# Layer 0: four of the six block sums of a group made by GpSimd from blocks on chip, in place of adding DMAs

## The chip, the cores and the metric

The kernel runs on one core of a Trainium2 chip. The core has a matrix engine (TensorE, PE in the profile), three engines that work on data in the on-chip memory SBUF (VectorE is DVE, ScalarE is ACT, GpSimd is POOL), a queue engine that issues DMAs (SyncE, SP), and 16 DMA engines. Matmuls write into a second memory, PSUM. The engines run side by side, each through its own list of instructions in order, and wait for each other by semaphores. The metric is the device time of one execution in microseconds. The kernel before takes 595.17 us, the median of three runs (594.85 to 595.21).

## The reference, cut to what matters

Four layers are applied to x of 8 batches, 256 tokens and 1024 features, each added to its input.

```python
x = x + L0(x)   # x @ W^T, plus 2 * gated low-rank experts (router, top 2 of 8)
x = x + L1(x)   # x @ W1^T + b + coeff[b] * (x @ (2*mask[b] - 1))
x = x + L2(x)   # x @ weight[id[b]]^T
x = x + L3(x)   # low rank, A[id[b]] and B[id[b]]
```

The change concerns layer 0 alone. Its main part is

```python
base = jnp.einsum('btd,od->bto', x, W)
h = jnp.einsum('btd,erd->bter', x, A)
lora_out = jnp.einsum('bter,bte,eor->bto', h, gates, B)
return base + SCALING * lora_out
```

## The kernel before, in words

**Precision.** All operands are float32. Each is split into a high part, rounded to the type that the matrix engine takes (fp32r), and a low part, the rest. A product is made as high by high, high by low and low by high. ScalarE makes the high part (the tile whi, line 304) and VectorE subtracts it from the source to make the low part (wlo, by the helper at line 69, called from `lows`, line 307). Line 69 is VectorE's two-operand helper, so nearly all of VectorE's work shows under it.

**Groups and Strassen's scheme.** The 8 batches are 4 pairs of 512 tokens. Layer 0 takes two pairs at a time, so there are two groups (g = 0 and 1). In a group the product W by x is a 2 by 2 block product with seven block multiplications in place of eight (Winograd's form of Strassen's method). A11 to A22 are the quadrants of W, with the identity added where a block lies on the diagonal (that adds x itself), and B11 to B22 those of x: the first index halves the features, the second is the pair. Eight sums are needed for the multiplications:

- S1 = A21 + A22, S2 = A11 - S1 (the opposite sign of the usual form, and T2 likewise), S3 = S2 + A22, S4 = A12 + S2,
- T1 = B12 - B11, T2 = T1 - B22 (made by VectorE, like S2), T3 = B22 - B12, T4 = T2 + B21.

S2 and T2 are VectorE subtractions. The six that the title counts are the others, S1, S3, S4, T1, T3 and T4. Every sum takes the memory of a block that is no longer needed (the dictionary in `quad`, line 197): S1 and S3 lie in A21, S2 in A11, S4 in A12, T1 in B11, T3 in B12, T2 and T4 in B21.

**How a sum is made before.** A DMA issued by GpSimd adds an array of HBM to a tile in SBUF (`add`, line 748, the accumulating form). For S3 and S4 ScalarE first copies S2 to the place (lines 757 and 762), for T1 and T3 it negates the block there (line 768). Then the DMA adds the other operand, read from HBM once more. For S1 and S3 GpSimd adds the identity to diagonal 128x128 blocks (`fold_quad`, `fold_block`, line 251). Each sum has two halves (h = 0, 1) of 128x1024 elements, and each half is one DMA of 512 KB. The adding DMAs are the queue q0 of the page.

**Slots.** The order of the work is written out by hand; the framework adds the waits. Group g has 16 slots in layer 0, two per entry of a list of products, the h of each being the half of the inner dimension:

```python
L0_PRODUCTS = [("A11", "B11"), ("A12", "B21"), None, ("S1", "T1"), ("S4", "B22"),
               ("S2", "T2"), ("S3", "T3"), ("A22", "T4")]
```

The third entry has no product: its slots (4 and 5) take B12 and B22 through the experts alone. A slot consists of `l0_slot`, which issues the evacuations of PSUM (`l0_evacuate`), then the high parts of blocks two slots ahead (HI_AHEAD = 4 items), the folds, the low parts of blocks about one and a half slots ahead (LO_AHEAD = 3), the extra work listed for the slot, and then the matmuls (`l0_main`). A block of weights and one of x are the two items of a slot. There are 5 buffers for high parts and 4 for low parts, so a part can't be made before the slot that frees its buffer is over. Seven evacuations bring the results from PSUM; some of them (VectorE additions of PSUM tiles to SBUF tiles, c in the profile) have to be done before the next slot may write the same tile.

The extra work is listed by `l0_works` with `at(s, ...)`: the sums; the router of a pair (13 small VectorE instructions, `router`, line 331); the weighing of the experts (`weigh`); gates brought to the layout of the matmuls by the TensorE (for p0 of group 0) or through HBM (`expand`, `gates_by_rank`); their high and low parts (ghi, glo, `split_gates`, line 420). p0 and p1 are the two pairs of a group. T1 is listed in slot 2 of group 0 and slot 1 of group 1, S4 in slot 4, T3 in slots 6 and 4, S3 in slot 7, T4 in slots 9 and 10. Entries with a negative number come either ahead of the slot's other work or, in `l0_mids`, behind its matmuls: in slot 3 of group 0 the router of p1 and the second half of S2.

**Queues.** SyncE issues the loads in the order in which they are written. GpSimd's queue holds the folds, the adding DMAs of layer 0 and some adding DMAs of layer 1 (line 281). In one queue an instruction that waits holds up all behind it.

After layer 0 of a group come layers 1, 2 and 3 of its two pairs (`unit_slot`), about 180 us of matmuls for group 0 before layer 0 of group 1.

Of the kernel before, what the change touches and what calls it, by code (L numbers as in the profile page):

```python
# [12 lines left out]
ALU = mybir.AluOpType  # L13
# [21 lines left out]
def kernel(ctx: ExitStack, tc: tile.TileContext, x, lang, coeff, ids,  # L35
# [14 lines left out]
    nc = tc.nc  # L50
# [15 lines left out]
    copy = nc.scalar.copy  # L66

    def tt(o, a, b, op):
        nc.vector.tensor_tensor(o, a, b, op)  # L69
# [99 lines left out]
    for g in range(2):  # L169
        s = 0  # L170
        for pr in L0_PRODUCTS:
            for h in range(2):
                if pr is None:
                    quad = ("B12", "B22")[h]
# [16 lines left out]
    def pair_of(g, j):  # L191
        return 2 * g + 1 - j
# [4 lines left out]
    def quad(g, name):  # L197

        where = {"S1": "A21", "S2": "A11", "S3": "A21", "S4": "A12",
                 "T1": "B11", "T2": "B21", "T3": "B12", "T4": "B21"}.get(name, name)  # L200
        if where[0] == "A":
            return [W0[g, where, h] for h in range(2)]
        i, j = int(where[1]) - 1, int(where[2]) - 1
        return [X[g][:, j, 4 * i + 2 * h:4 * i + 2 * h + 2, :] for h in range(2)]
# [48 lines left out]
    def fold_quad(t, h, eng=None):  # L253
        for k in range(2):
            c = (2 * h + k) * P
            fold_block(t[:, k, c:c + P], eng)
# [30 lines left out]
    flat = lambda ap: ap.rearrange("p a b -> p (a b)")  # L287
# [43 lines left out]
    def router(pairs):  # L331
        n4 = 4 * len(pairs)
        t = lambda nm, w: gp.tile([P, n4, w], F32, tag=nm, name=nm)
        lt = t("lt", 32)
        for i, p in enumerate(pairs):
            nc.vector.transpose(flat(lt[:, 4 * i:4 * i + 4]), pls.pop(p)[:, :P])
        lv = t("lv", E)
        np = len(pairs)
        tt(lv.rearrange("p (q n) e -> p q n e", q=np),
           lt.rearrange("p (q n) e -> p q n e", q=np)[:, :, :, :E],  # L340
           bias[:, pairs[0]:pairs[0] + np].rearrange("p q (o e) -> p q o e", o=1)
           .to_broadcast([P, np, 4, E]), ALU.add)
        revb = rev.to_broadcast([P, n4, E])

        def top(v, nm):
            mx = t(f"mx{nm}", 1)
            nc.vector.tensor_reduce(mx, v, AX.X, ALU.max)
            eq = t(f"eq{nm}", E)
            tt(eq, v, mx.to_broadcast([P, n4, E]), ALU.is_equal)
            tt(eq, eq, revb, ALU.mult)  # L350
            fi = t(f"fi{nm}", 1)
            nc.vector.tensor_reduce(fi, eq, AX.X, ALU.max)
            oh = t(f"oh{nm}", E)
            tt(oh, revb, fi.to_broadcast([P, n4, E]), ALU.is_equal)
            return mx, oh

        m1, oh1 = top(lv, "1")
        rest = t("rest", E)
        nc.vector.scalar_tensor_tensor(rest, oh1, -3.0e38, lv, ALU.mult, ALU.add)
        m2, oh2 = top(rest, "2")  # L360
        d = t("d", 1)
        tt(d, m2, m1, ALU.subtract)
        routed[tuple(pairs)] = lt, d, oh1, oh2

    def weigh(pairs):

        n4 = 4 * len(pairs)
        t = lambda nm, w: gp.tile([P, n4, w], F32, tag=nm, name=nm)
        lt, d, oh1, oh2 = routed.pop(tuple(pairs))
        ex = t("ex", 1)  # L370
        nc.scalar.activation(ex, d, AF.Exp)

        den = t("den", 1)
        nc.vector.tensor_scalar(den, ex, 1.0, 0.5, ALU.add, ALU.mult)
        wt1 = t("wt1", 1)
        nc.vector.reciprocal(wt1, den)
        wt2 = t("wt2", 1)
        tt(wt2, wt1, ex, ALU.mult)
        tt(oh1, oh1, wt1.to_broadcast([P, n4, E]), ALU.mult)
        tt(oh2, oh2, wt2.to_broadcast([P, n4, E]), ALU.mult)  # L380
        tt(lt[:, :, :E], oh1, oh2, ALU.add)
        for i, p in enumerate(pairs):
            gate4 = lt[:, 4 * i:4 * i + 4]
            if p == pair_of(0, 0):
                gxs[p] = gp.tile([P, 4 * E, R], F32, tag="lg", name=f"gx{p}", bufs=3)
                nc.vector.tensor_copy(gxs[p].rearrange("p (n e) r -> p n e r", n=4),
                                      gate4[:, :, :E].rearrange("p n (e o) -> p n e o", o=1)
                                      .to_broadcast([P, 4, E, R]))
                continue
            gxs[p] = gp.tile([P, P], F32, tag=f"gx{i}", name=f"gx{p}")  # L390
            nc.vector.transpose(gxs[p], flat(gate4))
# [3 lines left out]
    def expand(p):  # L395

        by_expert[p] = dram.tile([E, N], F32, tag=f"gates{p}", name=f"gates{p}")
        gx = gxs.pop(p)
        for g in range(4):
            nc.sync.dma_start(by_expert[p][:, g * P:(g + 1) * P], gx[32 * g:32 * g + E])  # L400
# [13 lines left out]
    def gates_by_rank(p):  # L414

        gts[p] = gp.tile([P, N], F32, tag="lg", name=f"gt{p}", bufs=3)
        src = by_expert.pop(p).rearrange("e (o t) -> e o t", o=1).to_broadcast([E, R, N])
        nc.sync.dma_start(gts[p], src)

    def split_gates(key, gt):  # L420
        hi = gp.tile([P, N], FR, tag="ghi", name="ghi", bufs=2)
        lo = gp.tile([P, N], FR, tag="glo", name="glo", bufs=2)
        copy(hi, gt)
        tt(lo, gt, f32(hi), ALU.subtract)
        gates[key] = hi, lo

    def gate(p):
        tt(gts[p], phs.pop(p), gts[p], ALU.mult)

    def gate_difference(g):  # L430

        a, b = (gts.pop(pair_of(g, j)) for j in range(2))
        tt(a, a, b, ALU.subtract)
        split_gates(("diff", g), a)
# [289 lines left out]
    def sub(g, o, a, b, h):  # L724
        q = [flat(quad(g, n)[h]) for n in (o, a, b)]
        tt(q[0], q[1], q[2], ALU.subtract)
# [12 lines left out]
    def l0_works(g):  # L739


        p0, p1 = pair_of(g, 0), pair_of(g, 1)
        w = {}

        def at(s, *fs):
            w.setdefault(s, []).extend(fs)

        def add(name, h, src):
            nc.gpsimd.dma_start(quad(g, name)[h], src, accum_op=ALU.add)

        def s1_add(h):
            fold_quad(quad(g, "S1")[h], h)
            add("S1", h, w0[1, 2 + h])

        def s3_add(h):
            t = quad(g, "S3")[h]
            copy(flat(t), flat(quad(g, "S2")[h]))
            fold_quad(t, h)
            add("S3", h, w0[1, 2 + h])

        def s4_add(h):
            copy(flat(quad(g, "S4")[h]), flat(quad(g, "S2")[h]))
            add("S4", h, w0[0, 2 + h])

        def less(h, name, j, i):

            t = flat(quad(g, name)[h])
            nc.scalar.mul(t, t, -1.0)
            add(name, h, x[pair_of(g, j)][:, 4 * i + 2 * h:4 * i + 2 * h + 2])

        def both(f, *args):
            return [lambda h=h: f(h, *args) for h in range(2)]

        def subs(o, a, b):
            return [lambda h=h: sub(g, o, a, b, h) for h in range(2)]

        def lb_parts():
            copy(lbs[0], lb_raw)
            tt(lbs[1], lb_raw, f32(lbs[0]), ALU.subtract)

        if g == 0:
            at(1, constants, *both(s1_add))
            at(2, *both(less, "T1", 1, 0), lambda: router([p0]))
            at(3, lambda: weigh([p0]), lb_parts, lambda: sub(0, "S2", "A11", "S1", 0))
            at(4, *both(s4_add), lambda: gate(p0))
        else:
            at(0, *both(s1_add))
            at(1, *both(less, "T1", 1, 0))
            at(3, *subs("S2", "A11", "S1"))
            at(4, *both(s4_add), lambda: gate(p0))  # L790
        at(-5 if g else 4, lambda: split_gates(p0, gts[p0]))
        if g == 0:
            at(5, lambda: weigh([p1]), lambda: expand(p1))
        else:
            at(1, lambda: router([p1, p0]))
            at(2, lambda: weigh([p1, p0]), lambda: expand(p0), lambda: expand(p1))
            at(3, lambda: gates_by_rank(p0))
        at(6, lambda: gates_by_rank(p1))
        at(4 if g else 6, *both(less, "T3", 1, 1))
        t2 = subs("T2", "T1", "B22")  # L800
        at(7, t2[0], *both(s3_add))
        at(-8, lambda: gate(p1))
        at(8, lambda: split_gates(p1, gts[p1]), t2[1])
        at(10, lambda: gate_difference(g))
        for h in range(2):
            at(9 + h, lambda h=h: add("T4", h, x[p0][:, 4 + 2 * h:6 + 2 * h]))
        for i in range(4):
            at(12 + i, lambda i=i: split_c(p1, i))
        return w
# [328 lines left out]
    b = NB - 1  # L1138
    at, xt = l3[b // 2], xts[b]
# [88 lines left out]
```

## Time and profile before

| what | value |
|---|---|
| median of three runs | 595.17 us |
| the profiled execution | 595.89 us |
| its span (first to last instruction) | 594.0 us |
| TensorE busy | 586.2 us, 3388 matmuls |
| VectorE busy | 468.5 us, 561 instructions |
| ScalarE busy | 379.0 us, 449 instructions |
| GpSimd busy | 127.2 us, 178 instructions |
| layer 0 of group 0, matmuls | about 5 to 110 us |
| layer 0 of group 1, matmuls | about 292 to 398 us |
| DMA, queue of SyncE (q1) | 112.14 MB |
| DMA, queue of GpSimd (q0) | 16.78 MB |
| granted TensorE clock | 0.999 |

A row of the list in order of time reads: start in us, busy us, engine, line, operation, output<-inputs, shape, count, and in brackets how long the engine was idle before it and what ended that. In the names, A is a quadrant of W or a sum in its place, x a block of x or a sum in its place, c the result area of layer 0 (at first it also holds raw low-rank weights), lb a part of the experts' second matrix, ph the PSUM tile of the experts' first product, mm and po the PSUM tiles of layer 0 and of layers 1 and 2.

### The profile page before, as it was taken

How to read it: one execution, taken by the hardware profiler on the slowest of the kernel's cores; microseconds unless marked ns; L12 is line 12 of the kernel's file. 1: busy time of each engine (PE TensorE's matmuls, PEld its weight loads, DVE VectorE, ACT ScalarE, POOL GpSimd, SP SyncE). 2: the span in 40 equal slices, each digit the busy share in tenths (PEclk: the TensorE clock that was granted, in tenths of full speed). 3: DMA queues.
4: the chain of work that ended last, by engine and by line, in shares of the span. 5: the costliest groups of instructions: out<-in, count | busy, mean ns of one | idle time of the engine just before them, and what ended most of it. 6: DMA issues, size and time to landing. Idle time of an engine off the chain costs nothing.

```text
span 594.0 us, 9230 instructions
## 1 busy us (share of the span) xinstructions
PE 586.2 (99%) x3388; PEld 501.3 (84%) x3388; DVE 468.5 (79%) x561; ACT 379.0 (64%) x449; POOL 127.2 (21%) x178
## 2 busy tenths in 40 slices
PE   9999999999999999999999999999999999999995
PEld 8878788888888888888888888888888888888884
DVE  7687788899689999586647786889977999976753
ACT  5658466687659887544544865668866789864331
POOL 2313170113121013112210234211422210511000
PEclk9999999999999999999999999999999999999999
DMA  8977994567685876499913799835858586845704
GB/s 292 345 169 156 222 273 146 199 242 261 199 287 178 302 265 244 167 352 346 276 26 98 165 271 237 236 108 212 311 176 271 198 292 223 317 144 184 224 1 141
DMA packets 39878, 130.02 MB, mean 219 GB/s; under 512 B 4922, under 2 KB 6682, under 8 KB 39066
## 3 DMA queue, kind: packets, MB, share of 16 engines
q1 hardware_dynamic: 34938, 112.14, 54.0%
q0 software_dynamic: 4608, 16.78, 15.1%
q8 instruction: 26, 0.43, 0.3%
q10 hardware_dynamic: 288, 0.52, 0.3%
q14 instruction: 18, 0.15, 0.1%
HBM read 120.99 MB, written 8.44 MB: 218 GB/s over the span
## 4 chain that ended last, share of the span: by engine, by line
PE 88%; DMA 7%; DVE 2%; issue 1%; SPq 1%; ACT 0%; DVEq 0%; ACTq 0%
PE po L663 60%; PE mm L663 22%; DMA c<-in_lb 2%; DMA gt<-gates 2%; DMA A<-in_w 1%; DVE wlo L69 1%; DMA c<-in_la 1%; PE pb L473 1%; PE pf L502 1%; PE ph L692 1%; PE ph L693 1%; PE pl L326 1%; PE ph L694 1%; DMA gates<-gx 0%; PE pb L540 0%
## 5 line engine op out<-in xcount | busy, mean ns | idle before, releaser
L663 PE MATMUL po<-hl,whi 128*128 128x512 f32 x1016 | 243.7, 391 | 0.0
L663 PEld LDWEIGHTS po<-hl,whi 128*128 128x128 f32 x1016 | 186.4, 188 | 35.8
L69 DVE TENSOR_TENSOR wlo<-raw,whi 128x1024 fp32r<-128x1024 f32 x128 | 159.1, 1250 | 8.0 <-issue 7.5
L304 ACT CAST whi<-raw 128x1024 fp32r<-128x1024 f32 x128 | 133.7, 1047 | 19.1 <-PE mm L663 8.0
L663 PEld LDWEIGHTS po<-hl,wlo 128*128 128x128 f32 x1016 | 130.7, 191 | 6.2 <-issue 1.2
L663 PE MATMUL po<-hl,wlo 128*128 128x256 f32 x1016 | 133.1, 283 | 0.0
L663 PE MATMUL mm<-whi,whi 128*128 128x512 f32 x224 | 87.8, 392 | 0.0
L663 PE MATMUL mm<-wlo,whi 128*128 128x512 f32 x224 | 87.2, 390 | 0.0
L273 ACT ACTIVATE raw<-raw,negc,c 128x1024 f32<-128x1024 int32 x64 | 79.5, 1243 | 10.5 <-DMA raw<-in_mask 10.3
L251 POOL TENSOR_TENSOR raw<-raw,ident 128x128 f32<-128x128 f32 x72 | 54.3, 756 | 125.7 <-DMA raw<-in_w 115.7
L69 DVE TENSOR_TENSOR raw<-raw,w 128x1024 f32<-128x1024 f32 x56 | 69.5, 1240 | 1.1 <-issue 1.1
L663 PE MATMUL mm<-whi,wlo 128*128 128x512 f32 x224 | 70.3, 389 | 0.0
L251 POOL TENSOR_TENSOR w<-w,ident 128x128 f32<-128x128 f32 x28 | 27.7, 990 | 165.1 <-DMA w<-in_w 126.9
L69 DVE TENSOR_TENSOR wlo<-x,whi 128x1024 fp32r<-128x1024 f32 (+1 forms) x38 | 44.1, 1170 | 13.4 <-PE mm L663 8.5
L636 ACT COPY c<-po 128x512 f32<-128x512 f32 (+1 forms) x34 | 18.8, 553 | 52.5 <-PE po L663 52.4
L663 PEld LDWEIGHTS mm<-whi,whi 128*128 128x128 f32 x224 | 42.2, 188 | 9.7 <-issue 0.8
L663 PEld LDWEIGHTS mm<-whi,wlo 128*128 128x128 f32 x224 | 42.0, 188 | 8.9
L663 PEld LDWEIGHTS mm<-wlo,whi 128*128 128x128 f32 x224 | 42.1, 188 | 8.5
L304 ACT CAST whi<-A 128x1024 fp32r<-128x1024 f32 x26 | 27.3, 1050 | 28.4 <-PE mm L663 18.5
L304 ACT CAST whi<-x 128x1024 fp32r<-128x1024 f32 x34 | 35.3, 1049 | 10.8 <-PE mm L663 9.1
L639 ACT ACTIVATE sum<-po,b_sb 128x512 f32<-128x512 f32 (+1 forms) x36 | 23.1, 642 | 29.6 <-PE po L663 29.6
L69 DVE TENSOR_TENSOR wlo<-A,whi 128x1024 fp32r<-128x1024 f32 (+3 forms) x37 | 37.5, 1028 | 4.5 <-ACT whi L304 4.4
(134 smaller groups left out, 492.5 us busy)
## 6 DMA issues: line engine op xcount, KB each, us to landing
raw<-in_mask SPq DMA_DIRECT2D x64, 512.0 KB
raw<-in_w SPq DMA_DIRECT2D x64, 512.0 KB
w<-in_w SPq DMA_DIRECT2D x28, 512.0 KB
out<-c SPq DMA_DIRECT2D x29, 256.0 KB
A<-in_w SPq DMA_DIRECT2D x14, 512.0 KB
x<-in_x SPq DMA_DIRECT2D x6, 1024.0 KB
A<-in_w POOLq DMA_DIRECT2D x12, 512.0 KB, 9.1
x<-in_x POOLq DMA_DIRECT2D x12, 512.0 KB, 9.2
```

The source lines that it names most:

```text
L69: nc.vector.tensor_tensor(o, a, b, op)
L251: (eng or nc.gpsimd).tensor_tensor(t, t, ident, ALU.add)
L273: nc.scalar.activation(f32(raws[n]), raws[n], AF.Identity, bias=negc[:, b:b + 1], scale=c2[:, b:b + 1])
L304: copy(prep_hi(i), flat(source(i)))
L326: mm(pls[p][32 * g:32 * g + 32, :P], wrs[:, k, :], X[a][:, j, k, g * P:(g + 1) * P], start=(k == 0), stop=(k == K - 1))
L473: mm(pb[c:c + 32, j * T:(j + 1) * T], l3b[b][:, k, :], xts[b][:, k, :], start=(k < 4), stop=(k >= 4))
L502: mm(po, l3[q][:, (m + i) * P:(m + i + 1) * P], rt, start=True, stop=True)
L636: copy(xs, po[:, :, T:])
L639: nc.scalar.activation(xs, po[:, :, T:], AF.Identity, bias=b1c)
L663: mm(*args, skip_group_check=True, **kw)
L692: mm(phs[p], hi, v[0][:, kk], start=(k == 0), stop=False)
L693: mm(phs[p], hi, v[1][:, kk], start=False, stop=False)
```

## The change

S3, S4, T1 and T3 are no longer made by a ScalarE pass and an adding DMA. One GpSimd tensor_tensor for each half makes the sum from two blocks that lie in SBUF: S3 = S2 + A22, S4 = A12 + S2 (in A12's own place), T1 = B12 - B11, T3 = B22 - B12. In both groups together that is 16 GpSimd instructions of 128x1024, in place of 16 ScalarE passes and 16 DMAs of 512 KB. S1 and T4 stay adding DMAs. S3's folds stay behind it, on GpSimd. The slots in which the sums are listed are unchanged.

```diff
+        def on_chip(o, a, op, b):
+            nc.gpsimd.tensor_tensor(*(flat(t) for t in (o, a, b)), op)
+
         def s3_add(h):
             t = quad(g, "S3")[h]
-            copy(flat(t), flat(quad(g, "S2")[h]))
+            on_chip(t, quad(g, "S2")[h], ALU.add, quad(g, "A22")[h])
             fold_quad(t, h)
-            add("S3", h, w0[1, 2 + h])
 
         def s4_add(h):
-            copy(flat(quad(g, "S4")[h]), flat(quad(g, "S2")[h]))
-            add("S4", h, w0[0, 2 + h])
-
-        def less(h, name, j, i):
-
-            t = flat(quad(g, name)[h])
-            nc.scalar.mul(t, t, -1.0)
-            add(name, h, x[pair_of(g, j)][:, 4 * i + 2 * h:4 * i + 2 * h + 2])
+            t = quad(g, "S4")[h]
+            on_chip(t, t, ALU.add, quad(g, "S2")[h])
+
+        def block_less(h, name, other):
+
+            t = quad(g, name)[h]
+            on_chip(t, quad(g, other)[h], ALU.subtract, t)
...
         if g == 0:
...
-            at(2, *both(less, "T1", 1, 0), lambda: router([p0]))
+            at(2, *both(block_less, "T1", "B12"), lambda: router([p0]))
...
         else:
...
-            at(1, *both(less, "T1", 1, 0))
+            at(1, *both(block_less, "T1", "B12"))
...
-        at(4 if g else 6, *both(less, "T3", 1, 1))
+        at(4 if g else 6, *both(block_less, "T3", "B22"))
```

## The prediction

> **What bounds the kernel.** I read the page's busy times first, then who waited for whom on TensorE, then the chain that ended last.
>
> ```profile
> PE 586.2 (99%) x3388; PEld 501.3 (84%) x3388; DVE 468.5 (79%) x561; ACT 379.0 (64%) x449; POOL 127.2 (21%) x178
> ```
>
> The waits of TensorE (us in total, times, longest):
>
> ```profile
> PE mm L663 <- ACT ghi L423: 0.3, 1, 0.3
> PE po L1155 <- DVE rt L451: 0.2, 1, 0.2
> ```
>
> The matmul stream has no hole: of 594.0 us TensorE is busy 586.2, and the rest is the first 1.1 us and the tail after 586. Inside, the waits view names one wait of 0.3 us in layer 0 and one of 0.2 us at the end. So work taken off ScalarE or the DMA queues can shorten the span by about 0.3 us plus hardly visible waits, some 0.5 us in all. It can lengthen it wherever something TensorE reads becomes late, and each such delay stays to the end, since a full stream never catches up. The question is how much spare time the feeding engines have at the places the change touches. The rows of group 0 in order of time, in the middle of layer 0, answer it (start, duration in us; wlo is the low half of a block made by VectorE, read by the matmuls as the third product):
>
> ```profile
> 31.76 1.05 ACT L778 CAST lb<-c 128x1024 fp32r<-128x1024 f32 x1 [1.78 <-DMA c<-in_lb]
> ...
> 38.11 1.22 DVE L69 TENSOR_TENSOR A<-A,A 128x1024 f32<-128x1024 f32 x1
> 39.24 2.35 DVE L69 TENSOR_TENSOR wlo<-x,whi 128x1024 fp32r<-128x1024 f32 x2
> ...
> 40.51 0.50 PE L693 MATMUL ph<-wlo,laghi 128*128 128x512 f32 x1
> ...
> 43.70 0.50 PE L663 MATMUL mm<-glo,lb 128*128 128x512 f32 x1
> ```
>
> The first wlo of 39.24 ends at about 40.4, and the matmul that reads it starts at 40.51 and shows 0.50 where its neighbours show 0.39 or 0.40. The low gates (glo, ended 43.65) are taken at 43.70, again with 0.50. VectorE is exactly on time here, with no reserve; in 24 to 48 us it is busy 20.2 of 24.
>
> **What goes.** Per group eight ScalarE passes (L757, L762, L768; median 1.04 to 1.05 us each, 8.4 us) and eight adding DMAs of 512 KB (POOL queue, 0.87 us to issue, 9.1 us median to landing). ScalarE was waiting in these stretches, and the summed blocks were ready before their casts. These removals are worth 0, and 0.3 us where the gates of p1 land at 61.6, with S3 and T3 adding beside them.
>
> **What comes.** Per group eight GpSimd tensor_tensor of 128x1024 f32. S3's folds and the S1 and T4 adds stay. The trace has no such instruction; its nearest row is the fold, 128x128, on the same engine:
>
> ```profile
> 19.88 0.89 POOL L251 TENSOR_TENSOR A<-A,ident 128x128 f32<-128x128 f32 x2 [8.08 <-DMA A<-in_w]
> ```
>
> 0.44 us for 128 elements; eight of these make at most 3.5 us. As GpSimd time this is harmless: that engine is busy 3.7 us of the 24 from 24 to 48, its other work there is one row of DMA issues after another, and an adding DMA took about 9 us. What matters is what it does to VectorE. Another stretch:
>
> ```profile
> 84.12 2.75 POOL L251 TENSOR_TENSOR A<-A,ident 128x128 f32<-128x128 f32 x2
> ...
> 85.08 1.48 DVE L69 TENSOR_TENSOR wlo<-A,whi 128x1024 fp32r<-128x1024 f32 x1
> 86.48 1.48 DVE L69 TENSOR_TENSOR hl<-c,hl 128x1024 fp32r<-128x1024 f32 x1
> 87.89 1.48 DVE L69 TENSOR_TENSOR wlo<-x,whi 128x1024 fp32r<-128x1024 f32 x1
> 89.29 1.21 DVE L69 TENSOR_TENSOR wlo<-A,whi 128x1024 fp32r<-128x1024 f32 x1
> ```
>
> Two folds that took 0.89 alone take 2.75, and each of three folds (the third starts at 86.84) lengthens one VectorE instruction by 0.26 us. They take turns. The instruction at 54.84, which reads PSUM and one SBUF operand, kept its 1.22 us under two folds. The Trainium skill ("SBUF — State Buffer", who interferes with whom) has the rule: a VectorE instruction with two SBUF inputs and a GpSimd one that reads SBUF exclude each other for the whole instruction. That speaks against the change: costed as hidden GpSimd time it is worth 0; by the rule each instruction also costs VectorE its hold. The hold: 0.26 us for 128 elements gives 2.1 us for 1024. The skill's "GPSIMD Engine Reference" (performance versus the Vector engine) has 4497 ns for 2048 elements, so an estimate of 2.25; the upper bound is the 3.5 above, the lower 0 (VectorE always first). I take 2.1, which both support.
>
> **Where it falls, group 0.** GpSimd now takes each sum as soon as its inputs are there, in its queue's order: T1 (2), S4 (2), T3 (2), S3 (2 with 4 folds). "Late" is against the times before.
> 1. T1: x arrives at 24.4 (ScalarE's cast of it starts at 24.40), so T1 holds the port 24.5 to 28.8, just when VectorE runs the router of p0 (24.05 to 27.1, 13 small instructions, 9 with two SBUF inputs). 4.2 less 0.3 of overlap, less VectorE's idle times, 0.8 at 27.1 and 1.1 at 31.7 (it waited for lb): S2's first half ends 2.0 late.
> 2. S4's first half can start exactly then and holds VectorE off the router of p1: 2.1 less 0.2 that runs beneath. S2's second half and the wlo after it are 3.9 late, and TensorE with them: **3.9**.
> 3. S4's second half goes in before the next wlo: 2.1 less 0.4 of slack (ended 41.6, read at 42.0): **1.7**.
> 4. T3's first half goes before glo: 2.1, less most of the 0.8 that VectorE idled for ghi: **1.0**.
> 5. T3's second half goes before the wlo of T1: 2.1 less 1.5 of slack (ended 44.8, read at 46.35), **0.6**; the wlo of S1 behind it ends 0.4 after its need: **0.4**.
> 6. S3's first half and two folds (2.6) go between the weighing of p1 and two wlo with some 2 us of slack: **0.6**.
> 7. S3's second half, two folds and the subtraction T2 go before VectorE's addition that empties the first PSUM tile (54.84), which TensorE must have at slot 8's start, 57.28; 1.2 us of slack are left: **2.4**.
>
> Sum 10.6 us. SP's queue is touched once: the gates of p1 (47.2) go out late with VectorE, and the mask loads behind them; these blocks are needed after 109.9, and everything shifts alike.
>
> **Group 1.** T1 can start when the logits have read x (300.2) and falls in VectorE's empty stretch (295.5 to 302.6): 0; without that cover 2 to 4 us. S4 and T3 come after S2:
>
> ```profile
> 320.81 2.35 DVE L69 TENSOR_TENSOR A<-A,A 128x1024 f32<-128x1024 f32 x2
> ...
> 325.84 2.36 DVE L69 TENSOR_TENSOR wlo<-x,whi 128x1024 fp32r<-128x1024 f32 x2 [1.26 <-issue]
> ...
> 345.20 1.21 DVE L69 TENSOR_TENSOR c<-mm,c 128x1024 f32<-128x1024 f32 x1
> ```
>
> S4's halves hold the port to 327.4 (1.6 after wlo wanted it), T3's first half to 330.7, so the second wlo ends at 331.9 and is read at 331.25: **0.6**. T3's second half before glo: **1.1**. S3's halves before the addition at 345.2, which has 1.6 us of slack: **2.0**. Sum 3.7.
>
> Together 10.6 + 3.7 - 0.3 = 14.0 us. The profiled execution took 595.89 with a span of 594.0; I add the delay to the span (608.0) and in the same way to the median of 595.17, as 1.9 lies around both spans: **609.2**.
>
> **Rivals.**
> - *Partly hidden, 597 to 600.* VectorE's order of turns favours it: GpSimd gets in only before instructions with slack, and only step 2 or step 7 and half of group 1 hold, 2 to 5 us. For it: VectorE idles 3.8 of 24 us. Against: its idle times lie before the place without reserve. Chance 0.12.
> - *No change, 595.2.* GpSimd loses each contest while VectorE has work, or a long instruction doesn't hold the port. VectorE keeps its times, and the sums are 10 us early anyway. Against: three folds out of three got in between back-to-back VectorE instructions. Chance 0.08.
> - *Faster, 594.6.* As before, but sixteen adding DMAs less let lb land before 31.76 and the gates before 61.6; the 0.3 us wait and the small ones (0.1 each at 40.51 and 43.70) go. It decides if a hold is under 0.6 us: the three before step 2's end then fit in the 1.9 us of idle time. Chance 0.04.
> - *Longer holds, above 617.* With 3.5 us each of some twelve binding holds adds 1.4, up to 626. Also the clock: "TensorE: Matmul & The Clock Gate" (Part 1) says that an idle window of about 3.4 us halves it; no run here shows such a gap (PEclk is full in every slice), and by steps 2 and 3 gaps of 3.9 and 1.7 us would be about that long, worth some 2 us if one matched a window. Chance 0.06.
>
> **Numbers.** My own case, 600 to 617, has 0.70. The range of 8 in 10 takes in half of the partly hidden case: 598.5 to 617. A change of 0.2 % (1.2 us) is about what can be told from none: slower 0.88, same 0.08, faster 0.04.
>
> **What would show it.** GpSimd instructions of 2.2 to 4 us with 128x1024, VectorE's two-input rows of 3.3 us beside them, PSUM-reading ones still 1.22; TensorE waits in 40 to 70 us summing to some 10 and in 325 to 350 to 4, released by VectorE's wlo, glo and c; the wlo now at 39.24 some 4 us later. Wrong if VectorE's rows keep 1.22 us, if T1 runs later than the router (then steps 1 and 2 shrink), or if GpSimd's sums are not waited for and still TensorE's gaps name them.

## The result, and the profile after

The changed kernel takes 612.09 us (median of six runs, 611.38 to 613.5) against 595.29 us before in the same comparison: 16.8 us longer, a ratio of 1.0282 (95 % interval 1.0264 to 1.0301). The forecast was 609.2 us, 14.0 us longer.

The page of the changed kernel, its span and busy times, and the slices of TensorE's granted clock:

```profile
span 610.4 us, 9187 instructions
PE 592.3 (97%) x3388; PEld 504.5 (83%) x3388; DVE 489.7 (80%) x561; ACT 363.9 (60%) x433; POOL 160.8 (26%) x178
...
PEclk9998999999999999999999899999999999999999
```

The span grew by 16.4 us. The same 3388 matmuls are busy 6.1 us longer, and the granted clock, without a dent before, now dips in two slices. VectorE's 561 instructions are busy 21.2 us longer, although none was added: it stands still inside instructions. Of the 6.1 us, 0.67 lie ahead of the first sum: in this execution TensorE's second and third matmul of layer 0 took 0.63 us each, where those of before took 0.39. That doesn't come from the change, since the run with a gap in T1 (below), which does the same up to there, starts without it. The rest of the span's growth is waiting. The waits of TensorE in the changed kernel (us in total, times, longest):

```profile
PE ph L693 <- DVE wlo L69: 4.6, 2, 4.2
PE pf L502 <- DVE c L69: 2.7, 1, 2.7
PE mm L663 <- DVE c L69: 2.2, 1, 2.2
...
PE mm L663 <- ACT whi L304: 0.7, 1, 0.7
PE mm L663 <- DVE wlo L69: 0.7, 2, 0.5
PE po L1156 <- DVE rt L451: 0.2, 1, 0.2
```

The first five rows are 10.9 us of waiting that was not there, nearly all for VectorE; the 0.3 us wait for ghi is gone. None is for a sum. The rows of group 0 in order of time, VectorE, GpSimd and TensorE together, answer to those shown of before:

```profile
24.46 5.05 POOL L756 TENSOR_TENSOR x<-x 128x1024 f32<-128x1024 f32 x2
...
25.00 4.57 DVE L69 TENSOR_TENSOR lv<-lt,bias 128x32 f32<-128x32 f32 x1
...
36.83 1.22 DVE L69 TENSOR_TENSOR A<-A,A 128x1024 f32<-128x1024 f32 x1
...
38.19 2.41 POOL L756 TENSOR_TENSOR A<-A,A 128x1024 f32<-128x1024 f32 x1 [8.68 <-DVE A L69]
...
38.30 2.34 DVE L69 TENSOR_TENSOR lv<-lt,bias 128x32 f32<-128x32 f32 x1
...
43.09 1.22 DVE L69 TENSOR_TENSOR A<-A,A 128x1024 f32<-128x1024 f32 x1
44.23 4.52 DVE L69 TENSOR_TENSOR wlo<-x,whi 128x1024 fp32r<-128x1024 f32 x2
...
45.50 0.80 PE L693 MATMUL ph<-wlo,laghi 128*128 128x512 f32 x1 [4.19 <-DVE wlo L69]
```

A VectorE instruction of 0.19 us in the router, lv, takes 4.57 us while the two halves of T1 run, and 2.34 us while S4's first half runs. S2's second half starts at 43.09 instead of 38.11, the wlo behind it at 44.23 instead of 39.24, and TensorE waits 4.19 us for it.

An instruction that reads PSUM and one SBUF tile is not held. Under the first half of S3 in group 1 (POOL) the pair of additions c keeps the 1.28 us that it takes before, and the low half behind it, with two SBUF inputs, stands until the sum is done:

```profile
348.18 2.41 POOL L756 TENSOR_TENSOR A<-A,A 128x1024 f32<-128x1024 f32 x1 [2.90 <-DVE wlo L69]
...
348.03 1.27 DVE L69 TENSOR_TENSOR c<-pf,c 128x512 f32<-128x512 f32 x2
349.22 2.45 DVE L69 TENSOR_TENSOR wlo<-x,whi 128x1024 fp32r<-128x1024 f32 x1
```

The windows view of the changed kernel around TensorE's wait of 4.19 us (columns: length, then busy time and count of PE, PEld, DVE, ACT, POOL, granted clock, DMA share, GB/s):

```profile
44.00:46.00 2.00, 0.50 (x1) 0.50 (x2) 2.00 (x3) 0.00 (x0) 1.56 (x1) 0.65 0.00 0
46.00:48.00 2.00, 2.00 (x6) 1.32 (x4) 2.00 (x1) 0.00 (x0) 2.00 (x2) 0.50 0.00 0
48.00:50.00 2.00, 1.62 (x4) 1.01 (x4) 1.35 (x2) 0.54 (x2) 2.00 (x1) 0.50 0.00 0
```

The same view in steps of 1 us, for PE alone, has the ends of this stretch and of a second one:

```profile
44.00:45.00 1.00, 0.00 (x0) 0.80 0.00 0
...
51.00:52.00 1.00, 1.00 (x5) 0.79 0.00 0
...
344.00:345.00 1.00, 0.59 (x2) 0.99 0.00 0
...
348.00:349.00 1.00, 1.00 (x5) 0.81 0.00 0
```

A mean of 0.80 at half speed means that 0.4 of the microsecond were halved. So the clock is halved from 44.6 to 51.4, for 6.8 us, and a second time from 345.0 to 348.4, for 3.4 us, behind the 2.73 us wait in group 1. The second costs half of its length, 1.7 us. The first would by the same count, its 1.3 us of waiting left out, cost 2.7 us; whether it does is a question for an experiment.

By group: the first VectorE instruction on layer 3's projection, early in group 1 (pblo), starts at 302.59 before and at 313.44 after. So group 0 costs 10.85 us and group 1 the other 5.55. How much of the 10.85 is the 0.67 of the start can't be told exactly; the run with a gap in T1, which starts without it, reaches slot 8 of group 0 only 0.35 us sooner (68.53 against 68.87), so most of it is taken up by the later waits.

### The profile page after: what moved, and what is told of

Its sections match the earlier page's. It is cut to its first block, busy times and chain, and to the rows that moved or that the text cites. A ratio compares the mean times of both kernels' runs of the same rounds, so it can differ in the third digit from the quotient of the medians.

```text
span 610.4 us, 9187 instructions
## 1 busy us (share of the span) xinstructions
PE 592.3 (97%) x3388; PEld 504.5 (83%) x3388; DVE 489.7 (80%) x561; ACT 363.9 (60%) x433; POOL 160.8 (26%) x178
## 4 chain that ended last, share of the span: by engine, by line
PE 88%; DVE 7%; issue 3%; POOL 1%; ACT 1%; DVEq 0%; POOLq 0%; ACTq 0%
PE po L663 58%; PE mm L663 24%; DVE wlo L69 3%; DVE lv L69 1%; PE pl L326 1%; PE pb L473 1%; PE pf L502 1%; PE warm L1095 1%; DVE c L69 1%; PE ph L692 1%; PE ph L693 1%; PE ph L694 1%; ACT whi L304 1%; POOL A L756 0%; POOL A L251 0%
## 5 line engine op out<-in xcount | busy, mean ns | idle before, releaser
L251 POOL TENSOR_TENSOR raw<-raw,ident 128x128 f32<-128x128 f32 x72 | 52.9, 737 | 128.8 <-DMA raw<-in_w 112.9
L69 DVE TENSOR_TENSOR wlo<-x,whi 128x1024 fp32r<-128x1024 f32 (+1 forms) x38 | 54.5, 1443 | 11.3 <-PE mm L663 7.4
```

What stands on the lines that cost most here:

```text
L251: (eng or nc.gpsimd).tensor_tensor(t, t, ident, ALU.add)
```

## The experiments

Each run is compared with the kernel before on the same chip; the times are medians.

**Is it GpSimd's reading, and not the sums?** The kernel before keeps all its adding DMAs and gets sixteen additions that nothing reads:

```diff
+        def extra(h, name):
+            a = flat(quad(g, name)[h])
+            nc.gpsimd.tensor_tensor(scratch, a, a, ALU.add)
...
-            at(2, *both(less, "T1", 1, 0), lambda: router([p0]))
+            at(2, *both(extra, "B12"), *both(less, "T1", 1, 0), lambda: router([p0]))
```

and likewise with S2 ahead of S4 and S3, and B22 ahead of T3.

> The kernel before, its sums by adding DMAs, plus sixteen GpSimd additions of 128x1024 into a scratch tile that nothing reads, started by the same blocks at the same places as in the changed kernel. Port theory: most of the 16.8 us come back although every sum is made as before, 608 to 613 us. Lateness theory: nothing waits for the additions, 595 to 597 us.

615.5 us, ratio 1.0328 (1.0305 to 1.0351). The whole loss is there, 2.5 us above the expected range, without one sum being made otherwise. So the loss needs neither late sums nor another order of loads. The excess has a place in the trace, at the start of group 1:

```profile
298.01 2.77 DVE L452 SCALAR_TENSOR_TENSOR a<-a,low_a,a3raw 128x1024 fp32r<-128x1024 f32 x1 [3.94 <-ACT a L459]
300.70 2.91 DVE L69 TENSOR_TENSOR wlo<-x,whi 128x1024 fp32r<-128x1024 f32 x1
```

The two additions in T1's place write no x, so they don't wait until the logits have read it. They run from 297.5 to 302.5 and hold two VectorE instructions that T1 itself, in VectorE's empty stretch, doesn't meet. TensorE waits 0.7 us for the second of these and 1.8 us for the low half behind it (laglo), and its clock is halved for 3.4 us. That is some 4 us, the 2 to 4 us that the prediction put on T1 of group 1 without its cover.

The same places with writes in place of reads:

```diff
+            nc.gpsimd.tensor_tensor(scratch[:, :8], a[:, :8], a[:, :8], ALU.add)
+            for _ in range(2):
+                nc.gpsimd.memset(scratch, 0.0)
```

> The kernel before plus, at the same sixteen places, a GpSimd addition of 8 elements and two memsets of 128x1024, which write SBUF and read nothing. Port theory with the skill's rule (it is the reads that exclude each other): VectorE's rows keep 1.22 us, 595 to 597 us. If any busy GpSimd holds VectorE off, in proportion to its time: 603 us or more.

594.8 us, ratio 0.9991 (0.9981 to 1.0001). Two rows of this kernel, one of GpSimd's memsets and, within it, two low halves of VectorE:

```profile
40.17 1.97 POOL L776 MEMSET scratch<- 128x1024 f32 x2
...
38.84 2.36 DVE L69 TENSOR_TENSOR wlo<-x,whi 128x1024 fp32r<-128x1024 f32 x2
```

Their 2.36 us is what two take alone. GpSimd busy for 2 us costs VectorE nothing if it only writes. The memsets also hold up the adding DMAs behind them in GpSimd's queue, as the additions did, so it wasn't that either. What costs is reading SBUF beside a VectorE instruction with two SBUF inputs.

**The change without its price.** Each on-chip sum is cut to its first 8 columns, so S3, S4, T1 and T3 are not formed:

```diff
         def on_chip(o, a, op, b):
-            nc.gpsimd.tensor_tensor(*(flat(t) for t in (o, a, b)), op)
+            o, a, b = (flat(t)[:, :8] for t in (o, a, b))
+            nc.gpsimd.tensor_tensor(o, a, b, op)
```

> The changed kernel with each of the sixteen on-chip sums cut to its first 8 of 1024 columns: the waits and the order stay, nearly all of the GpSimd work goes, and S3, S4, T1 and T3 are not formed. It shows what the removal of the ScalarE passes and the adding DMAs is worth without the price. Port theory and the prediction's first part: 0.3 to 0.5 us faster than before, 594.8 us. If the removal itself costs (load order, other waits): above 596 us.

594.8 us, ratio 0.9987 (0.9973 to 1.0). Sixteen ScalarE passes and sixteen DMAs of 512 KB less are worth 0.4 us (0 to 1.6 by the interval).

**The length of one hold.** Each sum in eight instructions of 128 elements:

```diff
+            for i in range(0, 1024, 128):
+                c = slice(i, i + 128)
+                nc.gpsimd.tensor_tensor(fo[:, c], fa[:, c], fb[:, c], op)
```

> The changed kernel with each GpSimd sum cut into eight instructions of 128 elements. Port theory: VectorE gets a turn after each piece, so no row waits for more than about 0.3 us at a time; the routers still lose some 2.5 us each, the long rows 0.26 each; about 601 us, and VectorE's longest rows near 1.5 us. Theory that the amount of GpSimd work or its lateness counts: pieces take 0.42 us each, 3.4 us a sum against 2.4, so 612 us or more.

602.1 us, ratio 1.009 (1.0058 to 1.0121), single runs from 596.8 (mean granted clock 0.997) to 603.2 (0.991): part of this spread is how much of the run had the halved clock. More GpSimd time and less loss: the theory of the amount of work falls. Rows of this kernel:

```profile
24.81 6.79 POOL L759 TENSOR_TENSOR x<-x 128x128 f32<-128x128 f32 x16
...
25.06 6.60 DVE L69 TENSOR_TENSOR lv<-lt,bias 128x32 f32<-128x32 f32 x1
...
40.40 0.40 DVE L69 TENSOR_TENSOR lv<-lt,bias 128x32 f32<-128x32 f32 x1
...
49.50 1.48 DVE L69 TENSOR_TENSOR wlo<-x,whi 128x1024 fp32r<-128x1024 f32 x1
```

The long rows take the 1.48 us foretold, and the second router is hardly held (0.40). The first is a miss: lv stands through all sixteen pieces of T1, and TensorE waits 4.49 us at the first wlo, as long as in the changed kernel. The gain lies behind that place, where the other waits of 6.8 us shrink to 0.6 and the clock isn't halved a second time.

**Does the port pass from hand to hand?** A memset of 128x512 between the halves of T1 in group 0:

```diff
+            if h == 0 and name == "T1" and g == 0:
+                nc.gpsimd.memset(scratch, 0.0)
```

> The changed kernel with a memset of 128x512 (a write, some 0.5 us) between the two halves of T1 in group 0. In the changed kernel one small VectorE instruction stood 4.57 us through both halves. If a waiting VectorE instruction gets the port when GpSimd doesn't ask for it at once, it now stands 2.3 us and goes in the gap, and later ones wait for the second half; the time stays within 2 us of 612 either way. If it still stands through both, near 5 us, the port isn't given up between them.

613.6 us in two runs. The router's rows:

```profile
25.04 2.45 DVE L69 TENSOR_TENSOR eq<-lv,mx 128x32 f32<-128x32 f32 x1
27.53 0.19 DVE L69 TENSOR_TENSOR eq<-eq,rev 128x32 f32<-128x32 f32 x1
...
27.97 2.36 DVE L69 TENSOR_TENSOR oh<-rev,fi 128x32 f32<-128x32 f32 x1
```

With the gap, the waiting instruction goes after the first half, and another waits for the second. The sum is the same 4.4 us. Why lv stood through back-to-back GpSimd instructions here, while other VectorE instructions got between such (the folds shown of before, and the same lv with the additions that nothing reads, held for 1.93 us and not for both), stays open.

**VectorE makes the sums itself.**

```diff
-            nc.gpsimd.tensor_tensor(*(flat(t) for t in (o, a, b)), op)
+            nc.vector.tensor_tensor(*(flat(t) for t in (o, a, b)), op)
```

> The changed kernel with the sixteen sums on VectorE in place of GpSimd, at the same places of the list. Port theory (a VectorE instruction with two SBUF inputs stands still for the whole of a GpSimd instruction that reads SBUF): no contention is left, each sum costs VectorE 1.14 us in its own order; some 3.5 us reach TensorE in group 0 and 2.5 in group 1, about 601 us. Lateness theory (the sums come late, or the load order without the adding DMAs is worse): as the changed kernel or later, 612 us or more.

609.4 us, ratio 1.0232 (1.0215 to 1.0249). Both expectations miss: there is no contention, each sum costs 1.14 us, and still 14.1 us are lost. The rows of TensorE that wait in it:

```profile
45.56 0.73 PE L663 MATMUL mm<-ghi,lb 128*128 128x512 f32 x2 [1.95 <-ACT ghi L423]
62.64 0.47 PE L663 MATMUL mm<-whi,whi 128*128 128x512 f32 x1 [1.30 <-DVE c L69]
...
339.59 1.09 PE L502 MATMUL pf<-rt,a 128*128 128x512 f32 x2 [3.27 <-DVE c L69]
359.75 0.47 PE L663 MATMUL mm<-whi,whi 128*128 128x512 f32 x1 [1.99 <-DVE c L69]
```

They lie at nearly the same places. The sums are listed just ahead of the gates of slot 4 and the additions that empty PSUM, and VectorE has no 2.3 us to spare there. These waits and one of 0.71 us at 314 are 9.2 us; the clock is halved three times behind them, for 3.4 us each, which costs 5.1 us. Together that is the loss. So exclusion is the way in which GpSimd's time becomes VectorE's; what sets the loss is that VectorE is short of time at these places, whoever takes it.

**Step 1 alone.** T1 of group 0 as before, the rest on chip:

```diff
-            at(2, *both(block_less, "T1", "B12"), lambda: router([p0]))
+            at(2, *both(less, "T1", 1, 0), lambda: router([p0]))
```

> The changed kernel with T1 of group 0 alone made as before (ScalarE pass and adding DMA). Port theory: step 1 goes, S2 of group 0 is on time again and the first wlo is late by the 2.1 us of S4's first half alone; TensorE's gap there is about 2 us, too short for the halved clock; the waits behind it grow a little in exchange, about 610 us. Clock theory (the halved clock after the long gap is a large part): the 3.3 us of it in group 0 go too, about 606.5 us.

610.8 us, ratio 1.0266 (1.025 to 1.0282), where the first theory put it; its interval overlaps that of the changed kernel. The waits of TensorE:

```profile
PE ph L693 <- DVE wlo L69: 3.6, 2, 1.9
...
PE mm L663 <- DVE c L69: 2.3, 1, 2.3
...
PE mm L663 <- DVE glo L69: 0.7, 1, 0.7
PE mm L663 <- DVE wlo L69: 0.7, 2, 0.6
```

The clock isn't halved in the first 60 us, and now the steps of the prediction stand one by one: 1.9 for the first wlo, 1.7 for the second, 0.7 for glo, 0.7 for the wlo of T1 and S1, 2.3 at slot 8. Group 0 costs 7.97 us (pblo at 310.56), 2.9 less than in the changed kernel, about what step 1 had made S2 late. The median is only 1.3 us lower: this trace is of the fastest of four runs (609.5, mean clock 0.995), and the two slowest, 611.4 and 611.5, have 0.993 and 0.989.

**What the halved clock in group 0 costs.**

```diff
+        if s == 5 and g == 0:
+            idle = bank(0, "idle")
+            for _ in range(36):
+                mm(idle[:, :P], ident, ident, start=True, stop=True)
```

> The changed kernel with 36 small matmuls of the identity put into TensorE's list ahead of slot 5 of group 0, where it waits 4.2 us for the first wlo; they fill about 4 us of that wait, so the clock should not be halved behind it. Clock theory: the 3.3 us lost to the halved clock come back, about 608.8 us. Port theory: TensorE, faster, only meets the next late halves (wlo at 48.7, glo at 51.5, wlo at 54.9), whose waits grow; about 0.2 us come back, 611.9 us. If the fillers overrun the gap, up to 0.5 us more.

612.8 us, ratio 1.0284 (1.027 to 1.0298). TensorE in this kernel:

```profile
40.21 8.20 PE L853 MATMUL idle<-ident 128*128 128x128 f32 x72
51.79 0.50 PE L663 MATMUL mm<-glo,lb 128*128 128x512 f32 x1 [0.18 <-DVE glo L69]
55.13 0.50 PE L663 MATMUL mm<-wlo,whi 128*128 128x512 f32 x1 [0.52 <-DVE wlo L69]
```

Each of the 36 calls became two matmuls, so the fillers ran twice as long as meant, 8.2 us, and overran the gap by some 3. The clock stayed full, yet TensorE reaches the wlo of slot 6 at 55.13, against 54.94 in the changed kernel. Three microseconds of useless work and a clock twice as fast both leave no trace: until about 55 us VectorE sets the pace, and steps 3 and 4 of the prediction are only hidden beneath the halved clock. (After the 2.2 us wait at 69 the clock was halved in this run, which it was not in the changed kernel.)

**Group 1.** On-chip sums there alone, group 0 as before (the functions of both kernels, chosen by g):

```diff
-            on_chip(t, t, ALU.add, quad(g, "S2")[h])
+            if g == 0:
+                copy(flat(t), flat(quad(g, "S2")[h]))
+                add("S4", h, w0[0, 2 + h])
+                return
+            on_chip(t, t, ALU.add, quad(g, "S2")[h])
```

> On-chip sums in group 1 alone, group 0 as before. If the two groups' costs simply add, as the traces' 10.9 us up to group 1 and 5.5 us after it say: 595.3 + 5.5 = 600.8 us. By the prediction's own sum: 599.0 us.

600.4 us, ratio 1.0086 (1.007 to 1.0101), 5.3 us more than before: the groups add. Then the pair of layer 3 matmuls, whose PSUM bank VectorE empties behind the delayed wlo, is moved, with a control:

```diff
-        mids.update({s: lambda: fill(1) for s in (3, 4, 5, 7)})
+        mids.update({s: lambda: fill(1) for s in (3, 4, 6, 7)})
```

> On-chip sums in group 1 alone (600.4 us), with layer 3's pair of matmuls that stood in the middle of slot 5 of group 1 moved to slot 6. In group 1 the 2.7 us wait belongs to that pair: its PSUM bank is emptied by a VectorE instruction behind the two delayed wlo. If it is the cause, that wait goes and with it the halved clock after it (about 1.9 us); the wlo and glo of slot 5 are then waited for, about 1.7 us by the prediction's sum: 597.5 to 599 us. If something else sets group 1's cost, 600.4 as before.

> Control: the kernel before with only that pair moved from slot 5 to slot 6 of group 1. Nothing waits for it there: 595.2 us by every theory.

599.6 us (1.0048 to 1.0085), and the control 595.4 us (0.9985 to 1.0005). The waits of TensorE with the pair moved:

```profile
PE mm L663 <- ACT whi L304: 1.8, 1, 1.8
PE ph L693 <- DVE wlo L69: 1.3, 1, 1.3
...
PE mm L663 <- DVE glo L69: 0.8, 1, 0.8
```

The wait for that bank is gone, and its 2.7 us come back at the wlo, at glo and in slot 8: 3.8 us in all, against 3.4 in group 1 with the pair in place. No clock was halved in this trace (with the pair in place it was, for 6.8 us), and the median fell by only 0.8 us, less than expected. The pair was where VectorE's lateness showed, not a cost beside it.

Last, T1 of group 1 alone on chip, which the prediction priced at 0:

```diff
-            at(1, *both(less, "T1", 1, 0))
+            at(1, *both(block_less, "T1", "B12"))
```

> The kernel before with T1 of group 1 alone made by GpSimd on chip, all else by adding DMAs. In the trace of the changed kernel its two instructions run from 309.9 to 314.6, in a stretch where VectorE has one instruction of 0.7 us to do. Port theory: no two-input instruction is in the way, 595.2 us, at best 0.3 less. Theory that each on-chip sum costs its share whatever runs beside it (16.8 us by eight pairs): 597.3 us.

595.6 us, ratio 0.9999 (0.9982 to 1.0017). The same two instructions of 2.4 us that cost some microseconds beside the router of group 0 cost nothing where VectorE has nothing to do.

## Why the prediction held, step by step

The last column is the run with T1 of group 0 by DMA, in which step 1 is left out and the clock in group 0 stays full.

| step | forecast, us | in the trace after | without step 1 |
|---|---|---|---|
| 1: S2's first half late | 2.0 | 2.85 (36.83 for 33.98) | left out |
| 2: first wlo | 3.9 | 4.99 late (44.23 for 39.24), 4.19 waited | 1.9 (forecast 3.9 less 2.0) |
| 3: second wlo | 1.7 | 0.38, under the halved clock | 1.7 |
| 4: glo | 1.0 | none, under the halved clock | 0.7 |
| 5: the wlo of T1 and S1 | 0.6 + 0.4 | 0.52 + 0.17 | 0.7 |
| 6: weighing of p1 | 0.6 | none | none |
| 7: the PSUM addition of slot 8 | 2.4 | 2.23 | 2.3 |
| group 0: halved clock | 0 | 2.7 | 0 |
| group 0: late at the start | 0 | 0.67 | 0 |
| group 0 | 10.6, less 0.3 | 10.85 | 7.97 (forecast 8.3) |
| group 1: second wlo and glo | 0.6 + 1.1 | 2.73, one wait, at the layer 3 pair | |
| group 1: the PSUM addition | 2.0 | 0.73 | |
| group 1: halved clock | 0 | 1.7 | |
| together | 14.0 | 16.4 | |

The mechanism was right: the hold, taken from 0.26 us of a 128x128 fold as 2.1 us, measured 2.15 (lv 2.34 less its own 0.19), and group 0 came within 0.6 us of its sum. In the changed kernel the parts can't be read one by one: the halved clock took the place of steps 3 and 4, as the filled gap shows, and since each step starts from VectorE's lateness, a wait that is missing at one place turns up at the next. Without step 1 they can, and there steps 2 to 5 and 7 are each within 0.3 us of the forecast. Only step 6 is missing, and step 1 was 0.85 too small. (Step 7's slack was 1.0 us and not 1.2: before, slot 8 starts at 57.05.)

The mis-sized term is the clock. The sum had none of it; it stood among the rivals at 0.06, with 2 us and an idle window of 3.4 us. In group 0 this was harmless, since VectorE was late behind the wait anyway. In group 1 a wait of 2.73 us was enough, and behind it nothing was late until slot 8, so that its 1.7 us are added to the end. That is most of the 2.8 us between forecast and measurement.

That the waits of group 1 came out right, 3.5 us for 3.7, is in part luck, for both places were wrong. The forecast left out the layer 3 pair, whose PSUM bank VectorE empties between the two wlo and glo. And the PSUM addition of slot 8 did not have the 1.6 us of slack given to it: before, it ends at 346.41 and the matmul that needs it starts at 346.68. What saved it is that S3's second half fell into time in which VectorE had nothing to do:

```profile
354.47 2.40 POOL L756 TENSOR_TENSOR A<-A,A 128x1024 f32<-128x1024 f32 x1 [2.06 <-DVE wlo L69]
...
356.25 1.70 DVE L69 TENSOR_TENSOR wlo<-x,whi 128x1024 fp32r<-128x1024 f32 x1 [1.86 <-PE mm L663]
```

The wlo was held 0.48 us, the two instructions behind it 0.26 each by the folds. That makes 1.0 late, less 0.27 of slack, and 0.73 was waited. (The list of waits names a ScalarE cast there, which ended last by the profile; before, the same cast ends at 347.49, when that matmul has long started.)

Of the rivals, "no change" had GpSimd lose the contest; it wins, and once holds a small VectorE instruction through two of its own. "Partly hidden" falls with its premise: VectorE's 1.9 us of idle time were used up, and 2.85 remained. "Faster" has its 0.4 us measured, in the kernel without the sums, and its interval reaches down to 0. "Longer holds" was right about the clock and not about the holds.

## What to carry to other kernels

Before an elementwise pass goes to GpSimd because it looks idle, look for the VectorE instructions with two SBUF inputs that will run beside it: each such pass is VectorE time, here about 2.15 us for 128x1024 elements, while one that only wrote cost nothing (ratio 0.9991). What that costs is read at the place and not from the busy share: the same 4.7 us cost nothing in VectorE's empty stretch and delayed everything where a low half was ready 0.1 us before its matmul. And work taken off queues that nobody waits for buys nothing, 0.4 us for 8 MB of DMA and 16 ScalarE passes here.

## What the runs showed of the hardware

- TensorE's granted clock was halved for 6.8 us behind a wait of 4.19 us and for 3.4 us behind one of 2.73 us, so gaps shorter than the window in the prediction suffice; in the run with the sums on VectorE one of 1.95 us did. In the clock records of these traces every halved stretch inside a kernel is 3.413 us long or twice that, and in the changed kernel the two start 88 times 3.413 us apart (44.6 and 345.0): as if time were cut into steps of that length, each judged as a whole. A wait of 2.23 us at the same place then has 1.86 us in one step in the changed kernel, where the clock stayed full, and 1.99 in the run with the filled gap, where it was halved. Both figures are estimates, counted in such steps from the halvings of the same trace. Where the limit lies isn't shown; in the run with the sums on VectorE 1.8 us were enough. Runs of one kernel that differ in where the steps fall then differ in time.
- A VectorE instruction of 0.19 us stood 4.57 us through two GpSimd instructions, and 6.60 us through sixteen short ones, without a turn between them. With two additions that nothing reads it was let in after the first (1.93 us), and a memset of 0.5 us between the two was enough too. What decides stays open.
- Two memsets of 128x1024 took 1.97 us on GpSimd and lengthened no VectorE row beside them. A GpSimd addition of that size took 2.40 us without contention, near the 2.25 us estimated.
